# The first graph's background: seven quarter products for the next queries, and a turned copy through DRAM

## The chip, the cores and the metric

The kernel runs on one core of a Trainium2 chip. A core has TensorE (PE: matrix products, with its own weight loads, PEld), VectorE (DVE), ScalarE (ACT), GpSimd (POOL) and SyncE (SP). The engines run at the same time, each through its own list of instructions in order, and wait for each other by semaphores. Transfers between DRAM and on-chip memory (DMAs) are issued here from SyncE's and from GpSimd's list. An issuing engine also waits in its own order, so what is behind a waiting or a late DMA is late too. The metric is the device time of one execution in microseconds (us).

## The reference

Two layers of a graph network with normalization first, for 16 graphs (B) of 1024 nodes (N) and 256 channels (C), all in float32.

```
h  = relu(layernorm(x))                       # first layer
A  = 2*| |sigmoid(c_j - c_i) - 0.5| - 0.5 |   # c: sums over channels; symmetrised
g  = relu((h^T @ (adj * A)) * para)           # the queries, 256 x 1024 per graph
k, v = h @ kv_w                               # keys and values
x  = x + softmax(q k^T * scale) @ v           # 4 heads of 64
h  = relu(layernorm(x))                       # second layer
agg = A_hat @ h                               # normalised adj + identity
x  = x + batchnorm(relu(batchnorm(agg @ W1^T + b1)) @ W2^T + b2)
```

The batch norms run over all graphs, so the last products can only be finished when all graphs are through the hidden layer.

## The kernel before

**The stream.** After a short start for graph 0, the kernel runs the attention of graph 0, 1, 2 and so on (`attention`). One graph has 16 steps. A step writes two score blocks on TensorE (L1081), takes the exponential on ScalarE (L1089), adds up the denominators on VectorE (L1110, L1113), and multiplies the probabilities of the step before with the values (L1124). Between the two, a generator `background(b)` issues pieces of other work for the next graphs. Each piece names a cost, and `attention` takes pieces until their sum has reached `due`, which rises evenly from step to step to `total`, a number written by hand. What is left over at a graph's end is issued at once. The lists of all engines are filled in this program order; no scheduler moves anything (`manual_schedule`). `weave(main, (i, side))` issues one item of each side after each item of the main generator, from its i-th on, and the rest of the sides at the end.

**What a graph needs.** `Norm` makes the layer norm and the sums c (statistics on VectorE, the power on GpSimd at L96 and L97, the scaling with relu on ScalarE, L368). `differences` spreads the sums over all partitions through DRAM. `weigh` makes the eight weight blocks adj * A of 128 x 1024: a difference (L508) and tanh (L516) on ScalarE, a product with the adjacency on VectorE (L495). The queries multiply h with these blocks. Keys and values need h turned (channels on partitions), two tiles `ht` of 128 x 1024, one per 128 channels; `keys_values` is 8 pieces: four products into keys, four into values. Each product contracts over both `ht` tiles.

**Two ways to each, already in the code.** `plain_queries` (L638 on) is the direct product: 16 pieces of four matmuls. `queries` (L537 on) splits h and the weights in quarters and makes seven products of quarters (14 pieces) with sums on VectorE: `combine` adds quarters of h into a tile `s1` (L534, L535), `take` subtracts weight blocks (L571), `first` to `seventh` add the products into the query quarters, and `finish` multiplies with `para` and applies relu. `transposed` (L412 on) turns h with TensorE's transposes, four of 128 x 128 to a PSUM bank, and ScalarE copies them out (L424, L430). `squares` and `gathered` turn h without TensorE:

```python
def squares(b):
    for k in range(CC):
        sq = p1.tile([P, N], F32, tag="sq", ...)      # one buffer
        nc.vector.transpose(sq..., hs["a", b]...)     # 32x32 squares
        nc.gpsimd.dma_start(out=hsq_d[b][:, k], in_=sq)
        for _ in range(3):
            yield 0.0
```

`gathered(b, k)` then reads the squares back from DRAM in the right order by four DMAs on SyncE's list (L452). From the second graph on, the background makes queries by quarters and turns the graph after the next by squares, in `summed` and `prepare`.

**The first graph's background.** `background(0)` is written apart, because it has more to do: `degrees` (row sums, column sums and the diagonal of the adjacency, for the second layer's normalization) loads the transposed adjacency in eight tiles; ScalarE sums each (L241) and VectorE takes its diagonal (L243, L244). `graph` builds the second layer's adjacency in the form that quarter products need, in eight parts, all on GpSimd: two loads (L267), up to two additions of the identity (L281), four subtractions of 128 x 256 (L286 to L291) and three stores to DRAM (L293 to L295). The loads of the next part are issued in the midst of a part. These stores are first read at the second graph's aggregation (L716).

Of the kernel before, what the change touches and what calls it, by code (L numbers as in the profile page):

```python
# [23 lines left out]
def gnn_two_layers_kernel(  # L24
# [13 lines left out]
    B, N, C = x.shape  # L38
# [60 lines left out]
    def layers(shifted):  # L99
# [51 lines left out]
        def weave(main, *sides):  # L151

            for i, cost in enumerate(main):
                for start, side in sides:
                    if i >= start:
                        cost += next(side, 0.0)
                yield cost
            for _, side in sides:
                yield from side

        def double(slots):

            for _ in slots:
                next(slots, None)
                yield 0.0
# [67 lines left out]
        def degrees():  # L233

            nc.vector.tensor_reduce(row, rows.rearrange("p q t -> p t q"), AX.X, ALU.add)
            ahead = [load_adj_t(t, "at") for t in range(2)]
            yield 0.0
            for t in range(NT):
                a = ahead[t]
                blk = a[:, t * P : (t + 1) * P]  # L240
                nc.scalar.activation(a, a, AF.Copy, accum_out=col[:, t : t + 1])  # L241
                db = p1.tile([P, P], F32, tag="s1", name=f"db_{t}")
                nc.vector.tensor_mul(db, blk, ident)  # L243
                nc.vector.tensor_reduce(diag[:, t : t + 1], db, AX.X, ALU.add)  # L244
                if t + 2 < NT:
                    ahead.append(load_adj_t(t + 2, "at"))
                yield 0.0
            nc.vector.tensor_add(deg, col, row)
            nc.vector.tensor_sub(deg, deg, diag)
            rsqrt(dinv, deg, 1.0, tmp_deg)  # L250
# [713 lines left out]
        def background(b):  # L964

            if b == 0:
                differences(1)
                for k in range(CC):
                    yield TOP
                    transposed(1, (k,))  # L970
                    yield 1.0
                w, products, norm = weighers[1], keys_values(1), Norm(2, True).all()
                yield from weave(islice(products, 4), (0, double(islice(w, 8))))
                asked, build, sums = plain_queries(1), graph(), degrees()
                yield from weave(
                    islice(asked, 13),
                    (0, w),
                    (4, norm),
                    (5, islice(build, 8)),
                    (7, islice(sums, 6)),  # L980
                )
                differences(2)
                yield from weave(asked, (0, build), (0, sums))
                w = weighers[2]
                yield from islice(products, 1)
                yield from weave(islice(products, 2), (0, islice(w, 2)))
                yield TOP
                transposed(2, (0,))
                yield 1.0
                yield from weave(islice(products, 1), (0, islice(w, 1)))  # L990
                yield from islice(w, 1)
                yield TOP
                transposed(2, (1,))
                yield 1.0
                yield from islice(w, AHEAD - 4)
                yield from products
                return
            before = hidden(b - 1)
            gather = aggregate(b - 1)
            if b + 1 < B:  # L1000
                w, products, norm = weighers[b + 1], keys_values(b + 1), normed(b - 1)
                yield from weave(islice(products, 4), (0, islice(w, 4)))
                asked = queries(b + 1)
                yield from weave(islice(asked, 7), (0, double(w)))
                if b == 1:
                    load_later()
                yield from weave(asked, (2, islice(norm, 5)))
                if b + 2 < B:
                    load_x(b + 2, True)
                yield next(gather)  # L1010
                yield from weave(products, (0, norm))
            else:
                yield next(gather)
                yield from weave(endings.pop(), (2, normed(b - 1)))
            if b + 2 < B:
                yield from weave(gather, (0, summed(b + 2)), (1, lately()))
                yield from prepare(b + 2, before)
            elif b + 2 == B:

                yield from weave(gather, (1, lately()))  # L1020
                endings.append(before)
            else:
                yield from weave(gather, (1, lately()))
                yield from weave(before, (0, normed_last()))
# [215 lines left out]
        def attention():  # L1240

            units = [Unit(b, k, f) for b in range(B) for k in range(CC) for f in range(NH)]
            steps = [(u, g) for u in units for g in range(NG)]
            per_graph = CC * NH * NG
            before = None
            at_top, at_mid, at_end, adds = {}, {}, {}, {}
            bg, done, total, top = iter(()), 0.0, 0.0, False
            for s in range(len(steps) + 2):
                if s < len(steps):
                    unit, g = steps[s]  # L1250
                    b = unit.at[0]
                    if s % per_graph == 0:
                        run(bg)
                        top = False
                        bg, done = background(b), 0.0
                        total = (37.6 if b > 0 else 41.0) * (b + 1 < B) + 24.0 * (b > 0) + 6.0 * (b == 0)
                        total += 12.0 * (0 < b < B - 2) + 25.7 * (b == B - 1) + 3.0 * (b == 0)

                        total -= 10.3 * (b == B - 1)
                    made = scores(*unit.at, g)  # L1260
                    due = total * (s % per_graph + 1) / per_graph
                    if b == B - 1:
                        due -= 0.5 * min(s % per_graph + 1, (per_graph - 1 - s % per_graph) * 0.75)
                else:
                    due += 5.1
                for action in at_top.pop(s, ()):
                    action()
                if top:
                    done += advance(bg)
                    top = False  # L1270
                for action in at_mid.pop(s, ()):
                    action()
                if s in adds:
                    adds.pop(s)()
                if s < len(steps):
                    for pr in made:
                        unit.add(pr)
                if before is not None:
                    (last, g_last), prs = before
                    last.values(g_last, prs)  # L1280
                    if g_last == NG - 1:

                        if last.closes:
                            last.fold(0)
                            last.fold(1)
                            at_top.setdefault(s + 1, []).append(last.sums)
                            wait = 1
                        else:
                            for e in range(2):
                                at_end.setdefault(s + e, []).append(lambda u=last, e=e: u.fold(e))  # L1290
                            opens = last.by_squares and last.at[1:] == (0, 0)
                            wait = 6 if opens else 4
                            at_mid.setdefault(s + 3 + opens, []).append(last.sums)
                        if last.by_squares:
                            at_top.setdefault(s + 2, []).append(last.gather)
                        else:
                            at_top.setdefault(s + wait, []).append(last.finish)
                        adds[s + wait] = last.add_output
                while done < due and not top:
                    cost = advance(bg)  # L1300
                    if cost is None:
                        break
                    if cost == TOP:
                        top = True
                        break
                    done += cost
                for action in at_end.pop(s, ()):
                    action()
                before = (steps[s], made) if s < len(steps) else None
            run(bg)  # L1310
# [402 lines left out]
```

## Time and profile before

| | |
|---|---|
| median of three runs (lowest to highest) | 2460.47 us (2459.99 to 2460.54) |
| the profiled execution, its span | 2460.34 us, 2458.6 us |
| TensorE, VectorE, ScalarE, GpSimd busy | 98%, 82%, 51%, 23% of the span |
| TensorE busy from 54 to 164 us | 109.5 of 110.0 us |
| VectorE, ScalarE, GpSimd busy in the same stretch | 77.4, 82.0, 61.3 us |
| the first graph's attention starts | 54.1 us |
| the third graph's keys start | 163.84 us |

A line of a timeline gives the start and the length in us, the engine, the line of the kernel, the operation, what is written and read, the shape and the count. TensorE carries out each float32 matmul of the program as two, so a piece of four shows as x8. `pg` is a query product, `pk` keys, `pv` values, `htp` a transpose, `sc` scores, `o` the product with the values, `sums` a small product for the denominators; `aht_d` and `hsq_d` are tensors in DRAM, `sq` the square transposes.

### The profile page before, as it was taken

The numbers are of one execution on the slowest core, as the hardware profiler recorded it, in microseconds if no ns is written. First come the engines' busy times: TensorE is split into PE (matmuls) and PEld (weight loads), VectorE is DVE, ScalarE is ACT, GpSimd is POOL, SyncE is SP. The second block draws the span as 40 slices with busy tenths as digits, with TensorE's granted clock in tenths as the row PEclk, the third lists the DMA queues.
The fourth block names the chain that finished last, engine by engine and source line by source line (L and its number), as shares of the span: only waits on it lengthen the run. The fifth ranks groups of instructions, "written<-read, shape, count | busy, mean of one in ns | idle before, by whom it ended". The sixth has DMA issues, their size and how long they took to land. (4 is left out here: it accounts for less than half of the span.)

```text
span 2458.6 us, 35932 instructions
## 1 busy us (share of the span) xinstructions
PE 2412.4 (98%) x13290; PEld 832.6 (34%) x13290; DVE 2003.9 (82%) x3103; ACT 1257.7 (51%) x1870; POOL 559.5 (23%) x645
## 2 busy tenths in 40 slices
PE   9999999999999999999999999999999999999994
PEld 4333333333333333333333333333333332334444
DVE  5678888988888888888898888888888878767775
ACT  7874554545464545445454546454454534335554
POOL 1381202111111212020211212121202103136652
PEclk9999999999999999999999999999999999999997
DMA  4675545363645554453536355544545353456559
GB/s 146 204 242 182 172 138 179 118 229 125 209 139 193 171 189 163 158 171 126 209 117 231 120 201 160 197 164 167 172 134 188 116 201 142 152 197 230 196 193 372
DMA packets 204553, 437.18 MB, mean 178 GB/s; under 512 B 21456, under 2 KB 96720, under 8 KB 200272
## 3 DMA queue, kind: packets, MB, share of 16 engines
q1 hardware_dynamic: 173328, 327.29, 39.7%
q0 software_dynamic: 31040, 107.50, 11.6%
q8 instruction: 107, 1.75, 0.3%
q14 instruction: 78, 0.64, 0.1%
HBM read 331.36 MB, written 103.35 MB: 177 GB/s over the span
## 5 line engine op out<-in xcount | busy, mean ns | idle before, releaser
L1089 ACT ACTIVATE p<-sc 128x1024 f32<-128x1024 f32 x512 | 495.4, 1020 | 649.5 <-PE sc L1081 649.5
L1113 DVE TENSOR_TENSOR acc<-acc,p 128x1024 f32<-128x1024 f32 x384 | 469.8, 1223 | 58.2 <-ACT p L1089 36.9
L1081 PE MATMUL sc<-q,k 64*64 64x512 f32 x4096 | 498.6, 602 | 0.5 <-ACT p L1089 0.5
L1124 PE MATMUL o<-p,v 128*64 128x512 f32 x2048 | 494.7, 604 | 0.0
L174 PE MATMUL pa<-aht,h_b 128*64 128x512 f32 x1536 | 346.0, 592 | 1.1 <-ACT h_b L368 1.1
L174 PE MATMUL pg<-w,x_h 128*64 128x512 f32 x1472 | 332.0, 592 | 0.0
L1081 PEld LDWEIGHTS sc<-q,k 64*64 64x64 f32 x4096 | 131.5, 132 | 336.4 <-issue 287.8
L1124 PEld LDWEIGHTS o<-p,v 128*64 128x64 f32 x2048 | 124.6, 136 | 297.7 <-issue 251.2
L1142 POOL DMA_DIRECT2D out_d<-os x58 | 32.9, 568 | 803.2 <-DVE os L1138 803.2
L495 DVE SCALAR_TENSOR_TENSOR w<-w,adj 128x1024 f32<-128x1024 f32 x128 | 164.9, 1288 | 46.1 <-ACT w L516 45.1
L174 PEld LDWEIGHTS pa<-aht,h_b 128*64 128x64 f32 x1536 | 110.1, 137 | 220.6 <-issue 207.8
L174 PEld LDWEIGHTS pg<-w,x_h 128*64 128x64 f32 x1472 | 105.7, 137 | 210.1 <-issue 198.4
L508 ACT ACTIVATE w<-cbc,csum 128x512 f32<-128x512 f32 x256 | 170.3, 716 | 0.0
L516 ACT ACTIVATE w<-w 128x1024 f32<-128x1024 f32 x128 | 135.6, 1059 | 2.5
L571 DVE TENSOR_TENSOR w<-w,w 128x1024 f32<-128x1024 f32 x112 | 134.6, 1232 | 1.5
L174 PE MATMUL pv<-kvw_f,ht 128*64 128x256 f32 x1024 | 116.1, 379 | 0.0
L174 PE MATMUL pk<-ht,kvw_f 128*64 128x512 f32 x512 | 115.2, 593 | 0.2 <-ACT ht L430 0.2
L174 PE MATMUL py<-at,w 128*64 128x512 f32 x464 | 112.6, 593 | 0.8 <-DVE at L729 0.7
L174 PE MATMUL py<-at,w1s 128*64 128x512 f32 x448 | 107.9, 595 | 0.0
L1453 ACT ACTIVATE yin_f<-yin_f,sm_f 128x512 f32<-128x512 f32 x128 | 93.5, 803 | 19.0 <-DMA yin_f<-y_d 17.0
L826 POOL DMA_DIRECT2D y_d<-y x112 | 61.6, 550 | 145.1 <-DVE y L846 75.8
L1160 DVE TENSOR_REDUCE part<-acc 128x16 f32<-128x512 f32 x128 | 87.8, 686 | 4.4
(197 smaller groups left out, 2968.6 us busy)
## 6 DMA issues: line engine op xcount, KB each, us to landing
aht<-aht_d SPq DMA_DIRECT2D x224, 512.0 KB
adj<-in_adj_dram SPq DMA_DIRECT2D x128, 512.0 KB
y_d<-y POOLq DMA_DIRECT2D x128, 256.0 KB, 3.0
yin_f<-y_d SPq DMA_DIRECT2D x32, 1024.0 KB
para<-in_para_dram SPq DMA_DIRECT2D x64, 256.0 KB
x_d<-x_x POOLq DMA_DIRECT2D x16, 1024.0 KB, 5.1
xo_f<-x_d SPq DMA_DIRECT2D x32, 512.0 KB
out_dram<-xo_f POOLq DMA_DIRECT2D x32, 512.0 KB, 11.1
```

Source lines behind the costliest of these rows:

```text
L174: nc.tensor.matmul(dst[r], left[:, r], right, start=start, stop=stop)
L495: nc.vector.scalar_tensor_tensor(w, w, 1.0, a, op0=ALU.add, op1=ALU.mult)
L508: nc.scalar.activation(w[:, t, :].rearrange("p (t q) -> p t q", q=P), cbc[:, q * NT // NH : (q + 1) * NT // NH], AF.Abs, bias=csum[:, th * ...
L516: nc.scalar.activation(made[i], made[i], AF.Tanh, scale=-0.5 / C)
L571: nc.vector.tensor_sub(block(i)[part], block(x)[part], block(y)[part])
L826: nc.gpsimd.dma_start(out=y1_d[i][:, j, :], in_=y)
L1081: nc.tensor.matmul(sc[part, e, :], ks[b][k][r, m * P + c * HW : m * P + (c + 1) * HW], qs[b][k][r, f * FB : (f + 1) * FB], start=True, sto ...
L1089: nc.scalar.activation(pr, sc, AF.Exp)
L1113: nc.vector.tensor_add(self.acc, self.acc, pr)
L1124: nc.tensor.matmul(self.o[r, :], vs[b][k][:, m, r], pr[:, e, :], start=(m == 0), stop=(m == NT - 1),)
L1160: nc.vector.tensor_reduce(self.part[:, e, :], acc.rearrange("p (c s) -> p c s", s=SQ), AX.X, ALU.add)
L1453: nc.scalar.activation(y, y, AF.Relu, bias=sh[:, j : j + 1], scale=scale[:, j : j + 1])
```

## The change

Both edits are in the background of the first graph and in its hand-written total. The second graph's keys and values are issued as a whole, ahead of its queries. The queries are the seven products of quarters. The third graph's norm, the graph's parts and the degrees begin with earlier pieces. The third graph's normed x is turned by `squares`, woven into the last pieces of the queries, and `gathered` once these are issued; its two calls of `transposed` are gone. The total of costs for the first graph goes from 50.0 to 43.6.

```diff
@@ background(0)
                 w, products, norm = weighers[1], keys_values(1), Norm(2, True).all()
-                yield from weave(islice(products, 4), (0, double(islice(w, 8))))
-                asked, build, sums = plain_queries(1), graph(), degrees()
+                yield from islice(w, 2)
+                yield from weave(products, (0, islice(w, 8)))
+                asked, build, sums = queries(1), graph(), degrees()
                 yield from weave(
-                    islice(asked, 13),
-                    (0, w),
-                    (4, norm),
-                    (5, islice(build, 8)),
-                    (7, islice(sums, 6)),
+                    islice(asked, 8),
+                    (0, double(w)),
+                    (0, norm),
+                    (1, islice(build, 7)),
+                    (3, islice(sums, 5)),
                 )
                 differences(2)
-                yield from weave(asked, (0, build), (0, sums))
                 w = weighers[2]
-                yield from islice(products, 1)
-                yield from weave(islice(products, 2), (0, islice(w, 2)))
-                yield TOP
-                transposed(2, (0,))
-                yield 1.0
-                yield from weave(islice(products, 1), (0, islice(w, 1)))
-                yield from islice(w, 1)
-                yield TOP
-                transposed(2, (1,))
-                yield 1.0
+                yield from weave(
+                    asked, (0, squares(2)), (0, build), (0, sums), (2, islice(w, 4))
+                )
+                for k in range(CC):
+                    gathered(2, k)
                 yield from islice(w, AHEAD - 4)
-                yield from products
                 return
@@ attention
-                        total = (37.6 if b > 0 else 41.0) * (b + 1 < B) + 24.0 * (b > 0) + 6.0 * (b == 0)
-                        total += 12.0 * (0 < b < B - 2) + 25.7 * (b == B - 1) + 3.0 * (b == 0)
+                        total = 37.6 * (b + 1 < B) + 24.0 * (b > 0) + 6.0 * (b == 0)
+                        total += 12.0 * (0 < b < B - 2) + 25.7 * (b == B - 1)
```

## The prediction

> **What bounds the kernel now.** I read the page first: the shares of busy time.
>
> ```profile
> PE 2412.4 (98%) x13290; PEld 832.6 (34%) x13290; DVE 2003.9 (82%) x3103; ACT 1257.7 (51%) x1870; POOL 559.5 (23%) x645
> ```
>
> An average over the span says little of one stage, so next came TensorE's waits in the stretch of the first two graphs' attention (54 to 320 us). There is one answer: half a microsecond.
>
> ```profile
> PE sc L1081 <- ACT p L1089: 0.5, 1, 0.5
> ```
>
> So TensorE never stops there, and each matmul removed is time gained, as long as nothing new makes it wait. Third, TensorE's timeline, for the work that is removed and the place where the third graph's keys begin (columns: start, length, engine, line, operation, out<-in, count):
>
> ```profile
> 72.88 1.89 PE L174 MATMUL pg<-w,x_h 128*64 128x512 f32 x8
> ...
> 150.10 1.09 PE L424 MATMUL htp<-ident,x_h 128*128 128x128 f32 x8
> ...
> 163.84 5.32 PE L174 MATMUL pk<-ht,kvw_f 128*64 128x512 f32 x24
> ```
>
> A piece of the queries (x8) holds TensorE for 1.72 us (three in a row start 1.72 apart), one column half's transposes for 1.03 (the next row starts at 151.13). The third graph's keys start at 163.84.
>
> Fourth, busy time by stretch (columns: stretch, length, PE, PEld, DVE, ACT, POOL busy, clock, DMA share, GB/s), because the change hands TensorE's work to VectorE and to GpSimd's DMA queue:
>
> ```profile
> 96.00:157.00 61.00, 61.00 (x396) 21.67 (x389) 47.35 (x72) 42.61 (x75) 53.66 (x65) 1.00 0.73 243
> 157.00:174.00 17.00, 17.00 (x101) 5.78 (x101) 13.77 (x15) 15.08 (x21) 16.60 (x20) 1.00 0.82 276
> ```
>
> Over the span GpSimd is at 23%; just here it is full: 53.7 of 61 and 16.6 of 17 us. Its timeline says with what: the eight parts of the aggregation's graph, from the first load to the last store.
>
> ```profile
> 96.35 1.67 POOL L267 DMA_DIRECT2D au_f<-in_adj_t_dram  x2
> ...
> 155.31 0.77 POOL L293 DMA_DIRECT2D aht_d<-au_f  x1
> 156.08 0.71 POOL L294 DMA_DIRECT2D aht_d<-two  x1
> 156.78 0.58 POOL L295 DMA_DIRECT2D aht_d<-one  x1
> ...
> 171.63 0.77 POOL L293 DMA_DIRECT2D aht_d<-au_f  x1
> 172.40 0.71 POOL L294 DMA_DIRECT2D aht_d<-two  x1
> 173.10 0.58 POOL L295 DMA_DIRECT2D aht_d<-one  x1
> ```
>
> The sixth part's stores end 61.0 us after the start, the eighth's 77.3. Nobody waits for this chain soon (the first load of what it stores is at 221.7), so its slowness costs nothing before.
>
> Last, what the route through DRAM costs where it is used already (graphs four onward): the square transpose, its store and the store's time to landing.
>
> ```profile
> L438 DVE STREAM_TRANSPOSE sq<-x_h x3: 1235/1236/1239, 262.4 to 396.8; 128x1024 f32<-128x1024 f32 x3
> ...
> L442 POOL DMA_DIRECT2D hsq_d<-sq x26: 555/588/629, 263.9 to 1885.4; - x26
> ...
> DMA to landing us min/median/max: 3.0/4.1/8.4
> ```
>
> **What the Trainium skill says.** "TensorE: Matmul & The Clock Gate", on the architecture (queue depths), calls the queues of ScalarE and VectorE strict FIFO: a waiting instruction holds up all behind it. The trace shows no counterexample. "SBUF — State Buffer", on the two separate sides, says VectorE and GpSimd share a port pair under an exclusive lock, taken by a VectorE operation with two SBUF inputs against a GpSimd one that reads SBUF. The trace agrees: the chain's 128x256 subtractions take 0.73 us or about 1.7, and the 1.73 one at 105.50 started 0.03 after a VectorE sum. "DMA: Bandwidth & Descriptors", on the anatomy of a GpSimd DMA, gives 2.0 us plus size by bandwidth, 3.2 for 512 KB; 4.1 measured here, and I use that. The clock-gate page also says a TensorE idle for some 3.4 us restarts at half clock for as long: an estimate of 1.7 lost. Before shows no such stall in mid-kernel, so it stays an estimate.
>
> **The change, part by part.**
>
> *Taken from TensorE.* Queries of graph 1: 14 pieces for 16, 2 x 1.72 = 3.43. Four column halves' transposes of graph 2, 2 x 1.03 = 2.06. Everything else up to the third graph's keys is only reordered. Without new waits they start at 163.84 - 5.49 = 158.35. The lower work total (50.0 to 43.6) only fits the smaller sum of pieces.
>
> *Added to VectorE.* Eight sums of weights at 1.23 (9.8), nine additions and four operations on quarters of x at about 0.68 (8.8), two square transposes at 1.24 (2.5): some 21 us in a stretch (66 to 158) with more than that free (18 of 24 and 47 of 61 busy). That alone is hidden by TensorE's pieces; I see one late spot, the sums of the second unit, about 2.5 us. ScalarE loses four copies and gains two of 0.6 and is not concerned. Keys and values ahead of the queries add nothing.
>
> *The DRAM route.* In the changed program's order, GpSimd's queue holds the first square's store behind the sixth part of the graph chain and the second's behind the eighth. The third graph's first key product contracts over both column halves, so it needs the second store, its gather, and thus the whole chain.
>
> When does that chain start? Its first load follows the norm's second piece, now with the second piece of the queries. Following order with the durations above: TensorE runs a step's scores and values in 3.64, so the sixth step's scores end at 94.5, ScalarE's exponentials at 96.8; VectorE then has two sums (98.3), one subtraction of weights (99.5), one weight product (100.7), statistics (101.7); GpSimd's power 1.3: first load at 103.0 for 96.35.
>
> Its length: 77.3 before. More two-input VectorE work in it (I count 29 of 47 us against 33 of 61) adds perhaps 1.6; the extra store 0.6; a halt of VectorE (next) gives back some 3.7 as the lock is free. 75.8: the second store issues at 178.8, lands at 182.9; SyncE issues four gathers at 0.43 (184.6). Their landing is not shown: at least 3.0 (the fastest store), at most 5.3 (gathers issued by 293.5 are read unwaited at 298.8); I take 3.5: 188.
>
> *A second wait, of VectorE.* The squares share one buffer, so the second transpose waits until the first store has landed: 103.0 + 47 (VectorE gets there at 150), store at about 162, landed at 166. Queued behind the waiting transpose on VectorE: the second graph's last query sums, and the attention's folds and sums, on which TensorE's sum product and, through the p buffers, ScalarE's exponentials wait. So TensorE stops first at the fifteenth or sixteenth step, from about 152 to 170, then has some 9 us left and reaches the keys by 179. This stall lies within the longer one. SyncE's queue holds the gathers behind the parameters' load, due about 177: not last.
>
> *Sum.* Keys at 188 instead of 163.84: +24.2; slow clock after the pause 1.5: +25.7. From there on the order is that of before, with VectorE and GpSimd caught up. The loads queued behind the gathers on SyncE (an adjacency block) are used some 15 us later. The profiled execution took 2460.34 (span 2458.6 and 1.7 around it), the median of the runs is 2460.47; so 2486.
>
> **Rivals.**
>
> *Hidden anyway: faster.* The store of the second square doesn't wait for the graph chain, or the chain is quick. Then the 5.5 of TensorE remains: 2455. To be hidden, the store must issue by 158.35 - 3.5 - 1.7 - 4.1 = 149, to break even by 154.5: a chain of 51.5 from 103.0. At the shortest durations shown, without any wait, it takes 56 (16 x 0.73 loads, 24 stores for 16.5, 32 x 0.73 and 8 x 0.45 subtractions, 1.3). Only another order could do it.
>
> *A shorter stall.* VectorE halts and GpSimd gets the port, nearing its shortest durations: chain 64, keys at 176, bounded below by TensorE's own way there: +12, 2472.
>
> *A longer one.* VectorE's added two-input sums lock GpSimd out in nearly each operation: 32 subtractions at 1.7 instead of a mean of 1.1 adds 19 at most, half of it likely: keys at 198, +36, 2496.
>
> *VectorE as the bound, no DMA wait.* The 21 us come through where they are not covered: 2460 + 5, if the stores were early. VectorE's free time in the stretch speaks against it.
>
> **How the numbers follow.** Main case 0.58 (2478 to 2491), shorter stall 0.17, longer 0.15, VectorE 0.03 (slower), hidden 0.07. About 0.2% is what a measurement of this kernel tells from no change (4.9 us). Hidden is faster by 0.22%, so mostly faster: 0.06, and 0.02 within. Slower: 0.92. The range reaches over most of both stall cases: 2470 to 2498; the unknown gather landing moves it by 2 only.
>
> **What would show it.** Right: in the changed profile TensorE idles about 30 us between 150 and 190, in two pieces, the last ended by the gathered columns; VectorE's second square waits 10 to 18 us for the first one's store; the second store starts near 179, behind the last graph part; queries are 14 pieces and no transposes of graph 2 appear. Wrong: the stores start near their transposes, or the chain starts at 96 as before, or it takes under 60 us. A later wait, after 190, for what the graph chain or SyncE delivers late would make it worse than I say.

## The result, and the profile after

The changed kernel takes 2487.87 us (median of 5 runs, 2486.56 to 2488.35) against 2460.47 (5 runs beside it, 2459.99 to 2460.55): ratio 1.0112, interval 1.0098 to 1.0125. The profiled execution took 2488.16 us, its span 2486.4: 27.8 more than before. The third graph's keys start at 191.18 us instead of 163.84, so 27.3 of the 27.8 lie ahead of them, in the first graph's attention.

The page's shares of busy time, after:

```profile
PE 2412.7 (97%) x13258; PEld 830.2 (33%) x13258; DVE 2024.2 (81%) x3126; ACT 1257.0 (51%) x1868; POOL 557.4 (22%) x647
```

TensorE has 32 instructions fewer (before 13290) and is busy as long as before. TensorE's waits from 54 to 320 us, after (what waits, for whom, total, times, longest; `group` is VectorE's step on a product for the denominators, whose PSUM bank the next query product takes):

```profile
PE sc L1075 <- ACT p L1083: 25.3, 4, 21.6
PE pg L174 <- DVE group L1175: 2.1, 1, 2.1
PE sums L1167 <- DVE part L1154: 0.6, 1, 0.6
```

Half a microsecond of waits has become 28. One wait holds most of it, and it is for ScalarE's exponentials, not for the gathered columns. TensorE's timeline, after (start, length, then what was idle before it and why):

```profile
121.30 2.62 PE L1075 MATMUL sc<-q,k 64*64 64x512 f32 x16 [2.55 <-ACT p L1083]
142.90 5.35 PE L174 MATMUL pg<-w,x_h 128*64 128x512 f32 x16 [2.08 <-DVE group L1175]
180.75 3.53 PE L1075 MATMUL sc<-q,k 64*64 64x512 f32 x16 [21.58 <-ACT p L1083]
191.18 5.33 PE L174 MATMUL pk<-ht,kvw_f 128*64 128x512 f32 x24
```

A score group of x16 otherwise takes 1.95 us and this row of query products 3.60; here they take 2.62, 5.35 and 3.53. The account of the keys' start is: 158.35 without new waits, 27.4 of waits (2.55, 0.59, 2.08, 21.58, 0.63), some 5.1 of matmuls stretched behind them: 190.9, and 191.18 is seen.

Who held the exponentials? ScalarE's timeline, after:

```profile
156.26 1.06 ACT L516 ACTIVATE w<-w 128x1024 f32<-128x1024 f32 x1
178.56 1.23 ACT L559 ACTIVATE q<-q 128x512 f32<-128x512 f32 x2 [21.24 <-DVE q L557]
179.70 1.92 ACT L1083 ACTIVATE p<-sc 128x1024 f32<-128x1024 f32 x2
```

The relu of two query quarters stands ahead of the exponentials in ScalarE's list, and waits 21.24 us for VectorE's product with `para`. VectorE's timeline, after:

```profile
140.93 1.23 DVE L438 STREAM_TRANSPOSE sq<-x_h 128x1024 f32<-128x1024 f32 x1
...
168.44 1.25 DVE L438 STREAM_TRANSPOSE sq<-x_h 128x1024 f32<-128x1024 f32 x1 [14.48 <-DMA hsq_d<-sq]
...
177.31 1.81 DVE L557 TENSOR_TENSOR q<-q,para 128x512 f32<-128x512 f32 x2
```

The second square transpose waits 14.48 us until the first one's store has landed, and VectorE then needs 7.6 us more for the list behind it until it comes to that product. And the store was late because of GpSimd's list, after:

```profile
103.14 1.67 POOL L267 DMA_DIRECT2D au_f<-in_adj_t_dram  x2
...
163.79 0.58 POOL L295 DMA_DIRECT2D aht_d<-one  x1
164.37 0.55 POOL L442 DMA_DIRECT2D hsq_d<-sq  x1
...
179.39 0.58 POOL L295 DMA_DIRECT2D aht_d<-one  x1
179.96 0.55 POOL L442 DMA_DIRECT2D hsq_d<-sq  x1
```

The first square was ready at 142.2 and its store issued at 164.4, right behind the sixth graph part; the second followed the eighth part. Busy time by stretch, after (the sums are those of PE, PEld, DVE, ACT and POOL in this order, then the clock, the DMA share and GB/s):

```profile
96.00:157.00 61.00, 55.77 (x308) 16.43 (x304) 55.39 (x80) 38.91 (x64) 46.80 (x56) 0.94 0.70 225
164.00:190.00 26.00, 8.62 (x52) 2.53 (x54) 19.95 (x25) 9.73 (x12) 18.22 (x23) 0.62 0.71 231
```

VectorE has gone from 47.35 to 55.39 of the same 61 us, although it stood still from 154 on. That is the second thing to explain.

### The profile page after: what moved, and what is told of

Same layout as the page of the kernel before. It is cut to its first block, busy times and chain, and to the rows that moved or that the text cites. A ratio compares the mean times of both kernels' runs of the same rounds, so it can differ in the third digit from the quotient of the medians.

```text
span 2486.4 us, 35895 instructions
## 1 busy us (share of the span) xinstructions
PE 2412.7 (97%) x13258; PEld 830.2 (33%) x13258; DVE 2024.2 (81%) x3126; ACT 1257.0 (51%) x1868; POOL 557.4 (22%) x647
## 3 DMA queue, kind: packets, MB, share of 16 engines
q8 instruction: 107, 1.75, 0.3%
## 5 line engine op out<-in xcount | busy, mean ns | idle before, releaser
L174 PE MATMUL pg<-w,x_h 128*64 128x512 f32 x1440 | 326.5, 595 | 2.1 <-DVE group L1175 2.1
L571 DVE TENSOR_TENSOR w<-w,w 128x1024 f32<-128x1024 f32 x120 | 145.5, 1241 | 1.5
L1104 DVE TENSOR_TENSOR acc<-p,p 128x1024 f32<-128x1024 f32 x64 | 78.1, 1220 | 17.2 <-ACT p L1083 17.2
## 6 DMA issues: line engine op xcount, KB each, us to landing
out_dram<-xo_f POOLq DMA_DIRECT2D x32, 512.0 KB, 10.9
```

Source lines behind the costliest of these rows:

```text
L174: nc.tensor.matmul(dst[r], left[:, r], right, start=start, stop=stop)
L571: nc.vector.tensor_sub(block(i)[part], block(x)[part], block(y)[part])
L1104: nc.vector.tensor_add(self.acc, self.held, pr)
```

## The experiments

Three causes stand at the start. **D**: the keys wait for the second square's store behind GpSimd's graph chain (the prediction's main case). **V**: VectorE's wait for the first store, passed on by ScalarE's list. **B**: VectorE is too full and would be late with no store in the way. Differences below are against the changed kernel, if nothing else is said. "No-wait time" is 2455.0, before less the 5.49 us of matmuls. The recorded expectations use other letters: there "theory G" is what is called D here, and in the runs e5, e6 and e7 "theory D" is what is called B here.

### Either of the two store waits alone

The second square of the third graph gets a buffer of its own (V gone, D left; run e1):

```diff
-                sq = p1.tile([P, N], F32, tag="sq", ...)
+                own = b == 2 and k == 1
+                sq = (p3 if own else p1).tile([P, N], F32, tag="ht" if own else "sq", ...)
```

> The second square of the third graph gets a buffer of its own; both stores stay on GpSimd's queue. Theory G (the second store behind the graph chain, then its gather, ends last): TensorE reaches the third graph's keys some 20 us earlier than it can have the columns, waits there, and the time stays at 2485 to 2494 (the chain gets no relief from a halted VectorE and may be some us longer). Theory V (VectorE's wait for the first store, with ScalarE's queue behind it, ends last): about 2465. If both end together, as the changed kernel's trace suggests (TensorE back from the one wait just as the columns land), removing one leaves the time where it is.

Measured: 2491.8 us, ratio 1.0125 (1.0108 to 1.0142). TensorE's waits, then GpSimd's and TensorE's timelines of this kernel:

```profile
PE pk L174 <- DMA ht<-hsq_d: 15.2, 2, 13.8
PE sc L1078 <- ACT p L1086: 12.2, 4, 7.1
```

```profile
185.74 0.55 POOL L445 DMA_DIRECT2D hsq_d<-sq  x1
```

```profile
194.76 7.38 PE L174 MATMUL pk<-ht,kvw_f 128*64 128x512 f32 x20 [13.77 <-DMA ht<-hsq_d]
```

With V gone, the keys' products over the first column half run at 179.91, and TensorE then waits for the second half's gathered columns, until 9.0 us after the second store's issue. D is real, and costs as much as V. The 12.2 us of waits for exponentials are nearly those of the kernel with both store waits gone (11.7, below), so they are no part of V.

The second store alone is issued by SyncE (D gone, V left; run e2):

```diff
-                nc.gpsimd.dma_start(out=hsq_d[b][:, k], in_=sq)
+                (nc.sync if b == 2 and k == 1 else nc.gpsimd).dma_start(out=hsq_d[b][:, k], in_=sq)
```

> The third graph's second store is issued from SyncE instead of GpSimd; VectorE still waits for the first store behind the sixth part of the graph chain. Theory V: TensorE stops and resumes as in the changed kernel, keys at about 191, time 2485 to 2490. Theory G: keys at some 170 to 175, time 2467 to 2472.

Measured: 2487.94 us, 1.0112 (1.0095 to 1.0129). TensorE's waits, and VectorE's timeline:

```profile
PE sc L1077 <- ACT p L1085: 25.5, 4, 22.1
```

```profile
168.56 1.25 DVE L438 STREAM_TRANSPOSE sq<-x_h 128x1024 f32<-128x1024 f32 x1 [14.92 <-DMA hsq_d<-sq]
```

V alone gives the whole loss too. With V alone the keys start at 191.32, with D alone their second part at 194.76. The two waits end within 4 us of each other, so taking one away gains nothing.

### Both store waits gone

SyncE issues both stores (`nc.sync if b == 2 else nc.gpsimd`; run e3).

> Both of the third graph's stores are issued from SyncE. Theories V and G alike: both long waits go, the keys come at 158.4 plus the small waits seen before the halt (2.6, 0.6 and 2.1 us) and their slow clock (3.5 us), at about 167: 2463 to 2464. The rival that VectorE's added work is the bound in any case, wherever the stores are: it catches up less without a halt, 2466 or more. The forecast of the hidden case, no small waits at all: 2455.

Measured: 2473.96 us, 1.0054 (1.0037 to 1.0071). 13.9 us are gained, and the time is still 19 above the no-wait time. TensorE's waits of this kernel:

```profile
PE sc L1075 <- ACT p L1083: 11.7, 4, 7.1
PE pg L174 <- DVE group L1175: 2.0, 1, 2.0
```

Busy time from 96 to 164 us, first of before, then of this kernel (the third sum is VectorE's):

```profile
96.00:164.00 68.00, 68.00 (x442) 24.43 (x436) 53.09 (x80) 49.58 (x84) 60.44 (x72) 1.00 0.74 246
```

```profile
96.00:164.00 68.00, 58.14 (x316) 17.10 (x312) 65.22 (x92) 39.67 (x66) 52.53 (x67) 0.94 0.73 248
```

VectorE is busy 65.22 of 68 us, and from 118 to 173 us its timeline has no gap. TensorE's longest wait, 7.1 us, is for exponentials that stand on ScalarE behind the relu of two query quarters, and this relu waits for VectorE's product with `para`, as in the changed kernel, but now with no store in the way:

```profile
163.85 1.23 ACT L559 ACTIVATE q<-q 128x512 f32<-128x512 f32 x2 [5.98 <-DVE q L557]
```

That is B. The keys start at 177.65, 19.3 us after 158.35: 13.4 of waits and some 5.3 of stretched matmuls make up nearly all of it. One group of the same kernel, from 96 to 178 us, tells a part of why VectorE is full:

```profile
L571 DVE TENSOR_TENSOR w<-w,w 128x1024 f32<-128x1024 f32 x8 | 12.0, 1517 | 0.0
```

The eight weight subtractions take a mean of 1.52 us here. I had put 1.23. In the changed kernel, where the mean is 1.40, the four that run singly, with no arithmetic on GpSimd beside them, take 1.22 each, and the two pairs take 3.14 and 3.03; beside the first pair run GpSimd subtractions of 1.71 and 1.60 us.

### Which edit costs

The first half of the change alone (run e4): quarters, keys and values first, and the side work earlier. The squares and their stores are gone altogether, and the third graph is turned by TensorE as before (total 45.6).

```diff
-                yield from weave(asked, (0, squares(2)), (0, build), (0, sums), (2, islice(w, 4)))
+                yield from weave(asked, (0, build), (0, sums), (2, islice(w, 4)))
                 for k in range(CC):
-                    gathered(2, k)
+                    yield TOP
+                    transposed(2, (k,))
+                    yield 1.0
```

> Only the first half of the change: keys and values first, queries by quarters, the third graph still turned by TensorE's transposes. If VectorE covers the quarters' sums (as forecast): 3.4 us gained, 2457. If the small waits of the changed kernel belong to the quarters: 5.2 us of waits and 3.5 us of slow clock against 3.4, so 2465 to 2466.

Measured: 2475.98 us, 1.0062 (1.0045 to 1.0079). TensorE's waits (`ot` is the transposes of a unit's output), then ScalarE's and VectorE's timelines:

```profile
PE sc L1075 <- ACT p L1083: 4.5, 3, 3.5
PE ot L1195 <- DVE q L595: 4.3, 1, 4.3
PE pg L174 <- DVE w L571: 4.2, 1, 4.2
```

```profile
155.13 1.06 ACT L241 ACTIVATE at<-at 128x1024 f32<-128x1024 f32 x1 [10.88 <-DMA at<-in_adj_t_dram]
120.25 0.69 DVE L357 SCALAR_TENSOR_TENSOR lnsm_a<-mv_a,lnsm_a 128x4 f32<-128x4 f32 x1 [6.74 <-POOL lnsm_a L97]
```

The third graph takes no DRAM route in this kernel, and it is 15.5 us slower than before: the first half of the change loses by itself. VectorE also stands 6.74 us here, waiting for the norm's power, which stands in GpSimd's list among the graph's parts. The new order of the side work without the quarters was not run, so how this loss divides between the two is not shown.

A further wait shows, of ScalarE's row sums for their adjacency loads. Two things make these loads late. SyncE issues them in its own order. They also share three buffers with the adjacency of the weight blocks, and VectorE frees these: with both stores on SyncE, SyncE waits 34.6 us in all for VectorE before row-sum loads (before: 30.6). A late load can thus be VectorE's lateness passed on.

The second half alone (run e6), squares on the kernel before: with `squares(2)` woven into the last three query pieces, stores on SyncE, `gathered` in place of the transposes, total 48.

> Only the second half of the change, on the kernel before: direct queries in the old place, the third graph turned by squares and DRAM, its stores on SyncE. TensorE saves the 2.06 us of the transposes; VectorE takes 2.5 us more. If VectorE has room without the quarters (theory D): 2458 to 2459. If the route through DRAM is late by itself at the end of the first graph: 2462 or more.

Measured: 2466.68 us (7 runs, 2466.18 to 2470.16), 1.0028 (1.0017 to 1.004). TensorE's waits, and ScalarE's timeline:

```profile
PE sc L1075 <- ACT p L1083: 4.1, 3, 2.4
PE pk L174 <- DMA ht<-hsq_d: 2.5, 1, 2.5
```

```profile
143.88 1.06 ACT L241 ACTIVATE at<-at 128x1024 f32<-128x1024 f32 x1 [10.12 <-DMA at<-in_adj_t_dram]
```

The last adjacency load of the row sums was issued at 135.62 by SyncE, behind the third graph's sums and a square's store; before, at 128.2. The time lies in the second expectation: this half loses in this order too, though less than the first.

### VectorE's instructions, the graph chain, or the row sums

Four kernels start from the one with both stores on SyncE. The graph's parts later (`(5, islice(build, 3))` for `(1, islice(build, 7))`; run e7):

> Both stores on SyncE, only the graph's parts on GpSimd begin later. Theory D with the lock and the wait for GpSimd's power as its main part: close to the run with both late, 2460 to 2467. If it is VectorE's own instructions that fill it: 2469 to 2474.

Measured: 2470.09 us, 1.004 (1.0025 to 1.0055); keys at 174.04 instead of 177.65. That is 3.6 us earlier, and the time lies in the second expectation. VectorE stays full (66.39 of 68 us from 96 to 164), and its eight subtractions still take a mean of 1.54 us, as the later chain still runs beside the two pairs. The gain is thus not in them. VectorE's 1.24 us wait for GpSimd's power is gone; where the rest comes from was not followed. Its own instructions bind VectorE more than the chain beside them.

The row sums later (`(6, islice(sums, 2))` for `(3, islice(sums, 5))`; run e8), and both later (run e5):

> Both stores on SyncE, only the degrees begin later. If VectorE's own instructions fill the stretch, some 3 us of them and their slow clock go: 2468 to 2471. If the lock and the wait for GpSimd's power are the main part: 2472 to 2475.

> Both third-graph stores on SyncE, and the graph's parts on GpSimd and the degrees begin later (from the sixth and seventh piece of the queries). Theory D (in the stretch from 116 to 178 us VectorE is full, from the quarters' sums, the degrees and the lock that GpSimd's subtractions take, and TensorE waits for it): VectorE gets back some 3 us of degrees, the 1.2 us wait for GpSimd's power and most of its lost lock time up to the queries' end, TensorE's waits shrink from 13.9 us by at least half and the slow clock with them: 2458 to 2466. If the waits come from the order of the quarters' products themselves, or only move later: 2472 to 2475.

Measured: 2477.92 (1.0075, 1.0059 to 1.009) and 2474.94 (1.0059, 1.0044 to 1.0075). With the row sums later the kernel is slower than with both stores on SyncE alone, a miss for both numbers of its expectation. With both later it is not told apart from that kernel (2473.96): the first expectation missed, the second, that the waits only move, holds. ScalarE's timeline with the row sums later:

```profile
163.54 1.06 ACT L241 ACTIVATE at<-at 128x1024 f32<-128x1024 f32 x1 [7.93 <-DMA at<-in_adj_t_dram]
```

The row sums are 5 to 6 us of VectorE work, but their place in ScalarE's list matters more: a late load holds the exponentials behind it. TensorE's longest wait grows from 7.1 to 11.3.

The weight subtractions of the second graph left out, to price B (run e11):

```diff
-                nc.vector.tensor_sub(block(i)[part], block(x)[part], block(y)[part])
+                if b != 1:
+                    nc.vector.tensor_sub(block(i)[part], block(x)[part], block(y)[part])
```

> The kernel with both stores on SyncE's list, and the eight subtractions of weight blocks of the second graph left out (its queries, and what follows from them, are then not the reference's: this measures VectorE's share alone). Theory (VectorE is the bound once the store's waits are gone): its list loses 8 x 1.23 = 9.8 us, and some of the stretched two-input operations: keys 10 to 13 us earlier than in that kernel's 177.65, time 2461 to 2464. Rival (the 19 us come from ScalarE's row sums that wait for late adjacency loads, or from slow clock, and VectorE is only busy beside them): within 3 us of 2474.

Measured: 2467.48 us, 1.0028 (1.0017 to 1.0039), between the two expectations: keys at 170.60, so 7.05 of the 19.3 us come back. Busy time and TensorE's waits:

```profile
96.00:171.00 75.00, 65.29 (x376) 19.48 (x374) 65.15 (x99) 49.51 (x78) 55.52 (x69) 0.98 0.81 264
```

```profile
PE sc L1076 <- ACT p L1084: 10.2, 5, 5.3
```

VectorE is at 65.15 of 75, no longer full, but ScalarE still waits for a load, with exponentials behind it, and VectorE itself waits for that row sum:

```profile
144.37 1.06 ACT L241 ACTIVATE at<-at 128x1024 f32<-128x1024 f32 x1 [5.80 <-DMA at<-in_adj_t_dram]
145.55 0.34 DVE L243 TENSOR_TENSOR db<-at,ident 128x128 f32<-128x128 f32 x1 [4.49 <-ACT at L241]
```

So B holds for part of the loss. Of the 12.0 us of subtractions left out, VectorE loses 4.49 again in this wait, and the 7.5 left are near the 7.05 gained. How the other 12.25 us divide between late loads and VectorE's remaining additions was not separated: ScalarE waited 10.1 us for query products and 5.8 for loads there, and some of both is covered.

### Three attempts at a faster version

Side work moved into the key and value products (run e12), where VectorE was free before (17.45 of 30 us busy from 66 to 96), again with both stores on SyncE:

```diff
-                yield from weave(products, (0, islice(w, 8)))
+                yield from weave(products, (0, islice(w, 8)), (2, islice(norm, 5)),
+                                 (3, islice(sums, 4)), (6, islice(build, 2)))
...
-                    (1, islice(build, 7)),
+                    (0, islice(build, 7)),
```

> The kernel with both stores on SyncE's list, and side work moved forward into the eight key and value products (66 to 96 us), where VectorE has over 12 us free and the DMA engines are used to 0.4: the third graph's statistics (2.9 + 1.2 + 1.3 = some 5 us of VectorE), the first three of eight row sums with their adjacency loads (2 us of VectorE, 3.7 of ScalarE), the graph's first load and first part. Theory (two causes are left in that kernel: VectorE's list is too full from 96 us on, and ScalarE's row sums wait for late adjacency loads, with the exponentials behind them): 7 us of VectorE go into free time and the last adjacency loads are issued earlier, keys 7 to 14 us earlier than 177.65, time 2460 to 2467. Rival (ScalarE, 24 of 30 us busy in 66 to 96, becomes late with the weights, and TensorE waits there instead): 2470 to 2476.

Measured: 2477.13 us, 1.0067 (1.0053 to 1.0081): slower than with both stores on SyncE alone (2473.96), near the rival's number but by another wait. VectorE's and ScalarE's timelines:

```profile
120.64 1.23 DVE L495 SCALAR_TENSOR_TENSOR w<-w,adj 128x1024 f32<-128x1024 f32 x1 [3.17 <-DMA adj<-in_adj_dram]
```

```profile
125.70 1.06 ACT L241 ACTIVATE at<-at 128x1024 f32<-128x1024 f32 x1 [11.33 <-DVE acc L1110]
```

The row sums' loads, moved forward on SyncE, pushed the last two weight blocks' adjacency back: issued from 108.05 to 114.9, where the kernel with both stores on SyncE issues them from 86.3 to 94.6. VectorE waited for one with the sums of the probabilities behind. ScalarE's next row sum waited 11.33 us for its own load, which SyncE could issue only at 121.89, when VectorE's product (the first line, ended at 121.87) had freed one of the three shared buffers. TensorE then waited 8.36 us.

Squares alone, but early (run e9): keys and values in one row, norm from the first query piece, squares at the ninth and twelfth, the graph's parts only behind their stores (`(12, islice(build, 1))`), total 48.

> The kernel before with the third graph's squares as the only gain (queries stay 16 plain pieces): norm from the first query piece, squares at the ninth and twelfth, both stores on GpSimd's list ahead of the graph's parts, which start at the thirteenth piece, keys and values in one row ahead of the queries as in the change, the columns gathered before the last query pieces; total of costs 48. If VectorE's 2.5 us of squares fit the gaps and the loads are early: 2 us of transposes gone, 2458.4, keys at 161.8. If the shift of the graph's parts or of the loads costs as in the run of the squares alone: 2462 to 2468.

Measured: 2485.65 us, 1.0105 (1.0088 to 1.0122). TensorE's waits, and VectorE's timeline 50 us further on:

```profile
PE pv L174 <- DVE q L605: 15.1, 1, 15.1
PE sc L1074 <- ACT p L1082: 5.7, 3, 4.4
```

```profile
242.12 0.69 DVE L557 TENSOR_TENSOR q<-q,para 128x512 f32<-128x512 f32 x1 [10.28 <-DMA para<-in_para_dram]
```

The graph chain now starts at 137 and its last stores are issued by 221. Its two load buffers are the ones that `load_later` fills next: the loads into them are issued at 216.57 and 236.03 (before: 178.67 and 189.76), and the parameters of the third graph's queries stand behind them on SyncE. Nobody reads the chain's stores sooner than before; its buffers are wanted. SyncE waits 31.8 us for the chain's store before the first of these loads. Before the second it waits 7.2 us for the power of the degrees, which stands behind the chain on GpSimd, and then 11.3 us until that power's store has landed.

Squares alone, in the order of need (run e10): graph parts at their old place, the last row-sum load ahead of the third graph's sums, squares woven into the pieces of the second graph's values, gathers right behind the values, three query pieces after them, stores on SyncE, total 49.

> The kernel before with only the third graph's squares in place of its transposes, and the lists of the issuing engines kept in the order of need: the last adjacency load of the row sums ahead of the third graph's sums, then the squares' stores on SyncE, all gathers as soon as the second graph's values are issued, the last three query pieces behind them, the graph's parts at their old place; total of costs 49. If the losses of the two earlier trials with squares alone came from that order (the late last row sum, the late gathers, the late graph parts): 2458.4 to 2459.5, at most 2 us below before, which is within the bound of what can be measured. If the route through DRAM has a cost of its own here that no order removes (the DMA engines are used to 0.7 to 1.0 in this stretch): 2463 to 2467, as in the first of the two trials.

Measured: 2463.2 us (21 runs, 2461.72 to 2468.52) against 2460.42: 1.0014 (1.0007 to 1.002), within 0.2% and yet slower, and in the second expected range. TensorE's waits:

```profile
PE sc L1079 <- ACT p L1087: 1.7, 2, 1.2
PE pv L174 <- ACT v L700: 1.5, 2, 0.7
```

The long waits are gone: neither ScalarE's row sums nor the keys wait for a load, so the reason given for that range, a cost of the DRAM route itself, is not shown either. What is left are 2.7 us of short waits more than before, where pieces stand differently between the steps; they are more than the 2.06 us of transposes saved. The span is 2.6 us longer, of which this explains 0.6; the rest was not followed. The DMA engines are used to 1.03 from 140 to 160 us in this kernel. No version was found that is faster than the kernel before.

## Why the prediction was right and wrong

**The total was right (2486 against 2487.87), as the main case, by one right cause and one missed.** That it fits to within 2 us is in part luck. The sum had no term for V's way to ScalarE, for the short waits or for their slow clock, but V happened to end together with D. Step by step:

*Taken from TensorE: right.* No transposes of graph 2, 14 query pieces; the account of the keys above closes to 0.3 us with 158.35 as its start. Two slips of words did no harm: the transposes are of two column halves (a row of x8 is one half), and the "8 x 0.45 subtractions" in the shortest chain are the additions of the identity.

*The DRAM route, D: right, with most of its sizes.* The chain starts at 103.14 (103.0), the first store is issued at 164.37 (about 162), the second at 179.96 (178.8). With V gone, the keys come 9.0 us after the second store, where I had 9.2 (4.1 to landing, 1.7 of issue, 3.5 for the gathers). The unknown gather time was well bounded. In the changed kernel itself the store landed later, after 6.5 us; the last gather was issued at 187.8, and the keys read the columns unwaited at 191.18, so D would have ended about there without V too. The relief of the chain by VectorE's halt was put at 3.7; it is 5.1: from its start to the second store's issue the chain takes 76.8 us with the halt and 81.9 without (the first experiment).

*The second wait, V: its length was right, what it leads to was wrong.* 14.48 us lies in my 10 to 18. But "this stall lies within the longer one" and "reaches the keys by 179" fell. I followed VectorE's list and left out ScalarE's. The relu of two query quarters waits there for VectorE, ahead of the exponentials, so TensorE had no 9 us of work between the two stalls. Where I expected it idle for about 30 us in two pieces, it stood in one piece of 21.6, from 159 to 181. V ended together with D, so the end was the same: two causes, each enough for the loss, as the first two experiments show. "TensorE's last wait is ended by the gathered columns" was therefore wrong in the changed kernel.

*"Hidden by TensorE's pieces", B: wrong.* This is the step that failed. One of its figures is misread: 18 of 24 us busy is VectorE from 140 to 164; from 66 to 96 it is 17.45 of 30. From 66 to 158 VectorE thus had 27.2 us free against 21 added, and the sum over the stretch was enough. What failed is where the free time lay. "Keys and values ahead of the queries add nothing" holds for TensorE, but it moves the first query piece from 72.88 to 90.88, and of the quarters' sums on VectorE all but the first two come after 96. From 96 to 164 VectorE had 68 - 53.1 = 14.9 us free; the other 12.6, from 66 to 96, were of no use. And a sum of 1.23 us takes longer beside GpSimd's chain, which makes the eight subtractions 12.0 us instead of 9.8. The Trainium skill, "SBUF — State Buffer", on the two separate sides, has the exclusive lock as the reason why such operations shut each other out; I had used it for GpSimd's lengths and not for VectorE's. The trace agrees: 1.22 for the single subtractions, 3.14 and 3.03 for the pairs in the changed kernel. So the rival "VectorE as the bound", given 0.03 and 2465, was the true state behind the stores, at 2473.96 and with no gap on VectorE for 55 us, and the first half of the change alone loses 15.5 us. The waits for the stores covered this.

*Left out altogether:* ScalarE's row sums wait for adjacency loads, whose issue depends on what stands ahead of them on SyncE and on when VectorE frees their buffers. Before, the longest such wait was 3.1 us and hidden; in ten of the twelve experiments it was 4.0 to 10.9, with the side work moved forward 11.3, behind a buffer that VectorE had to free, and only with squares in the order of need was there none.

*Slow clock: 1.5 put for one pause.* It was some 5 us in all, because the short waits before the long one cost as well (last section).

## What to carry to other kernels

Where a stall looks certain, follow it through the list of every engine that waits for the stalled one, and ask what stands ahead of the critical work in those lists: an in-order list turns a wait for a side job into a wait of the main job. Free time of an engine counts only where the added work can be done, with the length that the work has beside its neighbours there. And if two waits end together, an experiment that removes one of them shows no gain; only removing both shows what each was hiding.

## What the runs showed of the hardware

The prediction priced slow clock only behind the long stall. It had this from the Trainium skill, "TensorE: Matmul & The Clock Gate", part 1 on the clock gate, which puts TensorE at half clock after an idle window of some 3.4 us. The size agrees with the estimate of 1.7 us made from it, but the changed kernel shows the loss behind shorter waits too, and there the measurement decides. After 2.08 us of waiting, 5.35 instead of 3.60 (1.75 lost, granted clock 0.68); after 2.55, scores and the values product behind them took 2.62 and 2.97 instead of 1.95 and 1.94 (1.7 lost, 0.69); after 21.58, 3.53 instead of 1.95 (1.6 lost, 0.54). In the changed kernel, the long wait thus cost no more slow clock than a short one.

It is not so each time. In all fourteen kernels' traces, from 56 to 330 us, no wait of up to 2.01 us was followed by a loss. Of the 14 waits from 2.02 to 3.10 us, nine were followed by 1.6 to 1.8 us of loss and five by none; one of the five is a wait of 2.6 us at the same place in the kernel with only the second store on SyncE (2.00, granted clock 1.00). All 16 waits from 3.50 us up lost 1.5 to 2.9. Why some of the short ones cost and others do not is not shown.

VectorE's subtraction of two tiles of 128x1024 takes 1.22 us with no arithmetic of GpSimd beside it. Two of them in a row take 3.14 and 3.03 us in the changed kernel, and 3.83 and 3.29 with both stores on SyncE, beside GpSimd's graph chain, whose own subtractions of 128x256 take 0.73 us or about 1.7.
